# A gated graph network on one core: the z gate takes its third pass first, and the state is kept doubled

## The chip, the core and the metric

The kernel runs on one core of a Trainium2 chip. The core has a matrix engine (TensorE, PE in the profile, with its weight loads as PEld), a vector engine (VectorE, DVE), an activation engine (ScalarE, ACT), a general engine (GpSimd, POOL) and an engine that only issues transfers (SyncE, SP). TensorE writes its products into PSUM, here in eight banks of 128x512 float32; everything else lies in SBUF or in DRAM. The metric is the device time of one execution in microseconds, median of several runs.

## The reference

32 graphs of 512 nodes with 128 features each share one adjacency matrix `adj` of 512x512. Four layers follow each other, each as x = x + layer(relu(layernorm(x))). Layer 0 is a normalised graph convolution, layers 2 and 3 are graph attention. Layer 1, which the change is in, is a gated graph network of five steps:

```python
def step(h, _):
    m_in = jnp.einsum('nm,bmd->bnd', in_matrix, h)      # both matrices are adj
    m_out = jnp.einsum('nm,bmd->bnd', out_matrix, h)
    av = jnp.concatenate([m_in, m_out], axis=-1)
    u3 = h @ u3_w.T + u3_b
    z = jax.nn.sigmoid(av @ w3_w.T + w3_b + u3)
    r = jax.nn.sigmoid(av @ w4_w.T + w4_b + u3)
    hv = jnp.tanh(av @ w5_w.T + w5_b + (r * h @ u5_w.T + u5_b))
    h = (1.0 - z) * h + z * hv
    return (h, None)
```

All numbers are float32.

## The kernel before

**Products in three passes.** A float32 product would cost TensorE several passes. Most products here are made instead as three passes in a faster format (fp32r): both factors are cut into `upper` and `lower`, and a third operand `across` is made from the two (`operands`, L661 to L670: ACT makes upper at L664, DVE lower at L665 and across at L667). The first two passes add upper by upper and lower by lower into a PSUM bank. Then ACT multiplies the whole bank by SPLIT + 1 = 4097 in place (`rescale`, L672, instruction L673), and the third pass adds across by across. `in_three` (L675, passes at L691) does this for adjacency by state; `by_m` (L812, passes at L810) does it for the gates.

**A step.** `step` (L802) runs once for each graph and step, 160 times. In all but two of them the operands of the message m come in three parts ("split"). One PSUM bank serves the r gate and then the z gate: the z weights are loaded as the difference w3 - w4, so that the r gate's sum, with the part from the state in it, is the beginning of z's. After ACT has taken the tanh for r (L845), the bank is divided by 4097 (L849 and L850, an L673 instruction too), the first two passes of z follow, the bank is multiplied by 4097, the third pass follows, and ACT takes the tanh for z (L852). Sigmoids are taken as tanh of half the argument, so r and z stand here as 2 sigmoid - 1. The candidate has a bank of its own; its product with u5 (L807, a float32 product that stands as two matmul records in the profile) takes rh = (r + 1) h from L847, and u5 is halved for it. After its tanh (L856) DVE makes hv - h (L858), times z + 1 (L859), and half of that plus h (L861), the new state.

**Two layouts.** A state is needed features by nodes for the gates (hT) and nodes by features for the next adjacency product (h). Apart from the first few and the last, DVE transposes it in blocks of 32 into an `sq` tile (L642), SP writes this with four DMAs to DRAM (`far`, L645) and reads it back as whole rows (L647). The inputs of the steps (`shuttle_first`, L649) and of the attention layers go the same way. There are four sq buffers and four far buffers; the r, rh, z and hv tiles of all graphs share eight r buffers.

**Who runs when.** Nothing is written out in order. Every operation is announced to a `Plan` (L90) with its engine, a cost, a due time, the tiles that it reads and writes, and the delay until its result can be used. The plan plays this through with a limited number of buffers of each kind, always takes the most urgent operation that is ready on an engine, repeats this with other urgencies, shifts some of these by a list of numbers (`NUDGES`, L32) and then emits the instructions in that order. On the chip each engine runs its own queue in this fixed order. Six graphs (`LANES`) are in their steps at a time; the layers before and after are laid between them. [...] Two of the planned delays concern the change: the loads of x (L416) are reckoned with 3 us from their issue to the landing from the fifth graph on, and POOL's accumulating DMAs onto x (`add_onto`, L635) with 5.5.

**Normalisation.** `norm_relu` (L561) takes mean and variance on DVE (L553, L557), makes 1/sqrt(variance + eps) and -mean times this on POOL (L565 to L570), and ACT applies both with the relu (L572).

Of the kernel before, what the change touches and what calls it, by code (L numbers as in the profile page):

```python
# [32 lines left out]
    647971, 907480, 641022, 815328, 59938, 583104, 493449, 610727, 19299, 304899, 627144, 635903, 69303, 408061,  # L33
    213735, 192787, 7302, 58637, 834115, 963636, 6410, 705202, 955061, 53160, 882452, 878871, 458378, 231573,
    440371, 124696, 831158, 659333, 156550, 375431, 144007, 229366, 92171, 712320, 383813, 271697, 742240,
    798210, 397175, 163443, 123863, 724213, 516264, 896604, 122936, 743614, 457019, 570185, 62661, 920948,
    442263, 711198, 25011, 31858, 120261, 992683, 84663, 643357, 45247, 844390, 187975, 852865, 391757, 659128,
    736213, 659734, 397346, 484557, 410316, 685524, 527983, 521839, 433865, 543542, 868384, 394072, 205808,
    803310, 720274, 491124, 788541, 970038, 794737, 126558, 819621, 549318, 737826, 829243, 433351, 616176,
    868933, 314847, 688289, 939737, 907635, 853367, 672087, 953482, 982700, 636640, 260426, 745621, 974814,  # L40
    394689, 394423, 913904, 563868, 809734, 586161, 212429, 918084, 35227, 367565, 563487, 894884, 927872,
    820562, 407961, 31584, 797859, 266733, 239356, 49239, 168566, 825959, 690462, 633213, 766471, 952403,
    408935, 497281, 589831, 985192, 831666, 253050, 326020, 481827, 642272, 794393, 288155, 810682, 987219,
    726505, 745342, 441796, 26158, 800211, 187528, 795534, 149175, 951249, 42293, 197549, 962585, 253163,
    193842, 380099, 269941, 798210, 328761, 3598, 288464, 573452, 270841, 123133, 696935, 118976, 888464,
    549179, 731891, 706853, 313783, 900776, 668175, 816491, 294510, 923659, 444695, 534341, 679525, 202474,
    575303, 728118, 586387, 249556, 511121, 99992, 373622, 338542, 275589, 302881, 192606, 296189, 6121, 900716,
    93206, 158600, 419776, 382555, 10260, 855575, 704212, 698851, 696052, 457683, 55138, 404164, 139732, 866775,
    158170, 353170, 522421, 782841, 883529, 937879, 284896, 89904, 707913, 653847, 899032, 941515, 846706,
    471855, 178908, 722182, 666466, 211415, 810021, 295037, 269035, 402549, 983916, 571726, 473540, 395183,  # L50
    828707, 575084, 168839, 283291, 285134, 921509, 310987, 390552, 988218, 707221, 197452, 843224, 366926,
    884427, 545850, 986879, 832460, 861905, 777944, 317120, 973125, 261515, 931720, 503469, 106085, 519250,
    799711, 171717, 223192, 984270, 900296, 444443, 363172, 878758, 209540, 540746, 177829, 80204, 926590,
    322517, 646401, 549673, 224793, 442843, 438276, 448009, 366213, 419202, 112410, 62545, 971608, 549811,
    277513, 626388, 256930, 747343, 895280, 67763, 895530, 719737, 906641, 169362, 565633, 657856, 621526,
    269556, 28511, 630184, 65022, 38094, 940486, 350670, 532843, 24899, 947205, 540231, 223974, 479634, 329335,
    298114, 146538, 491725, 308524,
# [264 lines left out]
def gnn_stack(ctx: ExitStack, tc: tile.TileContext, a: dict, out: bass.AP):  # L322
# [13 lines left out]
    def flat(t):  # L336
# [8 lines left out]
        "sq": tiles(4, [P, Q, W * C], "sq"),  # L345
# [7 lines left out]
        "r": tiles(8, TOKENS, "r"),  # L353
# [43 lines left out]
    mhalf, eps, minus1 = (fixed(SMALL, k) for k in ("mhalf", "eps", "minus1"))  # L397
    warm = Val("r")
    op("POOL", 0.8, -1000, lambda: make_identity(nc, ident.t), w=[ident])
    for v, to in ((mhalf, -0.5), (eps, EPS), (minus1, -1.0)):  # L400
        op("POOL", 0.1, -999, lambda v=v, to=to: nc.gpsimd.memset(v.t, to), w=[v])
# [11 lines left out]
    for b in range(B):  # L413
        v = Val("x", C)
        op("SP", 0.5, -1002 if b == 0 else max(-995 + b, STEPS * b - 20) if b >= 8 else -995 + b,
           lambda v=v, b=b: nc.sync.dma_start(v.t, x[b].rearrange("(c p) d -> p c d", p=P)), w=[v], delay=(3.75, 5.2, 4.5, 5)[b] if b < 4 else 3)  # L416
        xs.append(v)
# [99 lines left out]
    gates = transposed((-9.5, -700, -700, -15.8), one(raw["u3"]), halves("w4"), halves("w3") + halves("w4", minus), halves("w5"), then=turned)  # L517
# [10 lines left out]
    u5T = transposed(-15.2, one(raw["u5"]), then=turned, by=0.5)  # L528
# [32 lines left out]
    def norm_relu(b, y, due, times=None):  # L561

        xb, off, rstd = xs[b], Val("off"), Val("rstd")
        mv = norm_stats(b, due)
        op("POOL", 0.5, due, lambda: nc.gpsimd.tensor_tensor(rstd.t, mv.t[:, :, 1], eps.t, ALU.add), r=[mv, eps], w=[rstd])  # L565
        op("POOL", 1.15, due, lambda: nc.gpsimd.tensor_tensor(rstd.t, rstd.t, mhalf.t, ALU.pow), r=[mhalf], w=[rstd])  # L566
        op("POOL", 0.42, due, lambda: nc.gpsimd.tensor_tensor(off.t, mv.t[:, :, 0], minus1.t, ALU.mult), r=[mv, minus1], w=[off])
        if times:
            op("DVE", 0.1, due, lambda: nc.vector.tensor_mul(rstd.t, rstd.t, times.t), r=[times], w=[rstd])
        op("POOL", 0.42, due, lambda: nc.gpsimd.tensor_tensor(off.t, off.t, rstd.t, ALU.mult), r=[rstd], w=[off], delay=2.6)  # L570
        for c in range(C):
            op("ACT", 0.385, due, lambda c=c: nc.scalar.activation(  # L572
                chunk(y, c), xb.t[:, c, :].rearrange("p (k j) -> p k j", k=Q) if y.kind == "h" else xb.t[:, c, :], AF.Relu, bias=off.t[:, c:c + 1], scale=rstd.t[:, c:c + 1]),
               r=[xb[c], off, rstd], w=[y[c * len(y.writers) // C]])
# [60 lines left out]
    def add_onto(x, what, reads, due):  # L635
        op("POOL", 1.0, due, lambda: nc.gpsimd.dma_start(x.t, what(), accum_op=ALU.add), r=reads, w=[x], delay=5.5)  # L636
# [147 lines left out]
    def ggnn(b, due):  # L784
        lane, h, hT = Val("lane"), Val("h" if b >= FAR0 else "y", C), Val("hT", Q)
        op("SP", 0.0, due - 3, lambda: None, r=[xs[b]], w=[lane], delay=0)
        op("SP", 0.0, due - 3, lambda: None, r=[lane], w=[h], delay=0)
        norm_relu(b, h, due - 2)
        if b >= FAR0:
            shuttle_first(h, hT, due - 2.5, due - 3)  # L790
        else:
            p = to_features(h, due - 2, hT)
            op("ACT", COPY, due - 2, lambda hT=hT: nc.scalar.copy(flat(hT.t), flat(p.t)), r=[p], w=[hT])
        for s in range(STEPS):
            now = due + LANES * s
            split = (b, s) not in WHOLE_GATES
            m = in_three(h, factors["adj"], now, split)
            if b == 4 and s == 0:
                op("SP", 0.0, now, lambda: None, r=[m[0] if split else m], w=[third], delay=0)
            h, hT = step(b, s, m, hT, now, lane)  # L800

    def step(b, s, m, hT, due, lane):  # L802
# [9 lines left out]
        def by_m(p, i, at, start, more=None, parts=None):  # L812
# [24 lines left out]
            op("PE", 2 * len(sums) * MR, at, first_two, r=[*of_gates[:2], *(v for _, three in sums for v in three[:2])], w=[p])  # L837
            rescale(p, at - 5)
            op("PE", len(sums) * MR + (MM if more else 0), at, third_one, r=[of_gates[2], *(three[2] for _, three in sums), *rest], w=[p])
# [9 lines left out]
        if split:  # L849
            rescale(gate, due - 5, 1 / (SPLIT + 1))  # L850
        by_m(gate, 2, due + 0.3, False)
        op("ACT", A, due - 5, lambda: nc.scalar.activation(flat(z.t), flat(gate.t), AF.Tanh, bias=gate_b["w3"].t, scale=0.5),  # L852
           r=[gate, gate_b["w3"]], w=[z])
        hv, new = Val("r"), Val("hT")
# [3 lines left out]
        op("DVE", V, due - 5, lambda: nc.vector.tensor_sub(flat(hv.t), flat(hv.t), flat(hT.t)), r=[hT], w=[hv])  # L858
        op("DVE", V, due - 5, lambda: nc.vector.scalar_tensor_tensor(flat(hv.t), flat(z.t), 1.0, flat(hv.t), op0=ALU.add, op1=ALU.mult),  # L859
           r=[z], w=[hv])  # L860
        op("DVE", V, due - 5, lambda: nc.vector.scalar_tensor_tensor(flat(new.t), flat(hv.t), 0.5, flat(hT.t), op0=ALU.mult, op1=ALU.add),  # L861
           r=[hv, hT], w=[new])
# [3 lines left out]
        if not EARLY <= due < STEPS * B:  # L866
            p = to_features(new, due + 2, *([] if last else [h]))
            if last:
                op("DVE", V, due + 2, lambda: nc.vector.tensor_add(flat(x.t), flat(x.t), flat(p.t)), r=[p, lane], w=[x])
            else:  # L870
                op("ACT", COPY, due + 1, lambda: nc.scalar.copy(
                    h.t.rearrange("p k (c j) -> p c k j", c=C), p.t.rearrange("p c (k j) -> p c k j", k=Q)), r=[p], w=[h])
            return h, new
        shuttle(new, "p (c q i) -> p q c i", h, due, due - 5)
        if last:
            mine = Val("y", 2)
            op("ACT", COPY, due + 2, lambda: nc.scalar.copy(
                mine.t.rearrange("p c (k j) -> p c k j", k=Q), h.t.rearrange("p k (c j) -> p c k j", c=C)), r=[h], w=[mine])
# [217 lines left out]
```

## Time and profile before

| | |
|---|---|
| median of 6 runs | 1498.71 us (1496.22 to 1501.37) |
| the profiled execution | 1496.22 us, span 1494.2 us |
| PE busy | 1486.3 us, 7464 matmul records |
| DVE busy | 1408.6 us |
| ACT busy | 1332.4 us, of which L673 466.4 us in 820 instructions of 599 ns |
| POOL busy | 447.7 us |
| DMA queues, share of 16 engines | SP's 40.6%, POOL's 16.1% |

The span runs from the first instruction to the last; the device time of the same execution is 2.0 us longer. A busy share says how long an engine had at least one instruction running. For PE it includes modelled ends, since matmuls overlap each other; the distance between the starts of matmuls in an unbroken run is the better measure of what one costs. The lists of waits name the waiting instruction, what released it, the total in us, the number of waits and the longest. PEld lines are weight loads, which run beside the matmuls. The granted clock of TensorE is at its full value from 6.3 us on to the end.

### The profile page before, as it was taken

The numbers are of one execution on the slowest core, as the hardware profiler recorded it, in microseconds if no ns is written. First come the engines' busy times: TensorE is split into PE (matmuls) and PEld (weight loads), VectorE is DVE, ScalarE is ACT, GpSimd is POOL, SyncE is SP. The second block draws the span as 40 slices with busy tenths as digits, with TensorE's granted clock in tenths as the row PEclk, the third lists the DMA queues.
The fourth block names the chain that finished last, engine by engine and source line by source line (L and its number), as shares of the span: only waits on it lengthen the run. The fifth ranks groups of instructions, "written<-read, shape, count | busy, mean of one in ns | idle before, by whom it ended". The sixth has DMA issues, their size and how long they took to land.

```text
span 1494.2 us, 25563 instructions
## 1 busy us (share of the span) xinstructions
PE 1486.3 (99%) x7464; PEld 1168.7 (78%) x7464; DVE 1408.6 (94%) x3323; ACT 1332.4 (89%) x2994; POOL 447.7 (30%) x636
## 2 busy tenths in 40 slices
PE   9999999999999999999999999999999999999999
PEld 7777777777787778777778777777777787777888
DVE  8989998999998998999999999999899999999898
ACT  6988998998989899999899989899989889989875
POOL 5411322222264223332324322333332214202321
PEclk9999999999999999999999999999999999999999
DMA  3345555745766567665665667666566565663233
GB/s 106 61 100 144 99 127 117 166 117 131 171 138 151 136 147 162 143 148 142 140 157 130 148 143 162 143 144 140 129 150 161 135 152 114 153 147 72 71 72 78
DMA packets 307499, 196.09 MB, mean 131 GB/s; under 512 B 87872, under 2 KB 259232, under 8 KB 307360
## 3 DMA queue, kind: packets, MB, share of 16 engines
q1 hardware_dynamic: 276160, 157.24, 40.6%
q0 software_dynamic: 30912, 36.71, 16.1%
q8 instruction: 59, 0.97, 0.3%
q14 instruction: 80, 0.66, 0.2%
q10 hardware_dynamic: 288, 0.52, 0.1%
HBM read 87.30 MB, written 70.37 MB: 106 GB/s over the span
## 4 chain that ended last, share of the span: by engine, by line
PE 57%; DVE 6%; DMA 1%; issue 1%; ACT 1%; SPq 0%; POOL 0%; DVEq 0%; ACTq 0%; POOLq 0%
PE bank L691 19%; PE bank L810 14%; PE bank L807 9%; PE bank L1001 9%; PE bank L932 3%; PE bank L987 1%; DVE e L975 1%; DVE lower L665 1%; PE bank L769 1%; DVE across L667 1%; DVE sq L642 0%; DMA h<-far 0%; DVE r L858 0%; DMA x<-y 0%; DVE r L859 0%
## 5 line engine op out<-in xcount | busy, mean ns | idle before, releaser
L673 ACT ACTIVATE bank<-bank 128x512 f32<-128x512 f32 x820 | 466.4, 599 | 50.5 <-PE bank L691 35.4
L667 DVE SCALAR_TENSOR_TENSOR across<-lower,upper 128x512 fp32r<-128x512 f32 x391 | 261.6, 679 | 2.4 <-PE bank L810 0.7
L810 PE MATMUL bank<-upper,gates 128*128 128x512 f32 x519 | 240.2, 463 | 0.1
L1001 PEld LDWEIGHTS bank<-h_gat,e 128*128 128x128 f32 x1792 | 220.3, 191 | 21.0 <-issue 11.7
L810 PE MATMUL bank<-across,gates 128*128 128x512 f32 x519 | 227.5, 466 | 0.6 <-ACT bank L673 0.5
L1001 PE MATMUL bank<-h_gat,e 128*128 128x129 f32 x1792 | 222.8, 275 | 0.0
L810 PE MATMUL bank<-lower,gates 128*128 128x512 f32 x519 | 205.0, 395 | 0.2 <-DVE lower L665 0.2
L691 PE MATMUL bank<-adj,across 128*128 128x512 f32 x640 | 188.3, 418 | 0.0
L691 PE MATMUL bank<-adj,upper 128*128 128x512 f32 x640 | 187.2, 414 | 0.0
L691 PE MATMUL bank<-adj,lower 128*128 128x512 f32 x640 | 175.4, 396 | 0.0
L636 POOL DMA_DIRECT2D x<-y x80 | 73.7, 929 | 313.5 <-ACT y L778 81.4
L565 POOL TENSOR_TENSOR rstd<-mv,eps 128x4 f32<-128x4 f32 x119 | 56.6, 476 | 369.8 <-DVE mv L557 361.5
L807 PE MATMUL bank<-r,wT 128*128 128x512 f32 x320 | 163.6, 593 | 0.4 <-DVE r L847 0.3
L975 DVE SCALAR_TENSOR_TENSOR e<-row,h_gat,maskT 128x512 f32<-128x512 f32 x224 | 157.3, 742 | 0.0
L566 POOL TENSOR_TENSOR rstd<-rstd,mhalf 128x4 f32<-128x4 f32 x119 | 150.6, 1266 | 1.5
L691 PEld LDWEIGHTS bank<-adj,across 128*128 128x128 f32 x640 | 117.5, 188 | 42.4 <-issue 12.5
L691 PEld LDWEIGHTS bank<-adj,upper 128*128 128x128 f32 x640 | 118.2, 188 | 37.0 <-issue 12.2
L691 PEld LDWEIGHTS bank<-adj,lower 128*128 128x128 f32 x640 | 120.5, 188 | 28.5 <-DVE lower L665 0.4
L810 PEld LDWEIGHTS bank<-across,gates 128*128 128x128 f32 x519 | 96.6, 188 | 48.4 <-ACT bank L673 19.2
L810 PEld LDWEIGHTS bank<-upper,gates 128*128 128x128 f32 x519 | 97.9, 189 | 38.0 <-issue 13.2
L845 ACT ACTIVATE r<-bank,gate_bw 128x512 f32<-128x512 f32 x160 | 111.2, 696 | 15.9 <-PE bank L807 15.5
L858 DVE TENSOR_TENSOR r<-r,hT 128x512 f32<-128x512 f32 x160 | 108.8, 681 | 15.9 <-ACT r L856 15.6
(153 smaller groups left out, 3069.7 us busy)
## 6 DMA issues: line engine op xcount, KB each, us to landing
far<-sq SPq DMA_DIRECT2D x936, 64.0 KB
h<-far SPq DMA_DIRECT2D x148, 256.0 KB
x<-y POOLq DMA_DIRECT2D x80, 256.0 KB, 4.2
sq<-far SPq DMA_DIRECT2D x56, 256.0 KB
row<-line SPq DMA_DIRECT2D x56, 256.0 KB
adjT<-y POOLq DMA_DIRECT2D x32, 256.0 KB, 4.2
hT<-far SPq DMA_DIRECT2D x120, 64.0 KB
x<-in_x_dram SPq DMA_DIRECT2D x24, 256.0 KB
```

Of the source, the lines that this page charges most:

```text
L565: op("POOL", 0.5, due, lambda: nc.gpsimd.tensor_tensor(rstd.t, mv.t[:, :, 1], eps.t, ALU.add), r=[mv, eps], w=[rstd])
L566: op("POOL", 1.15, due, lambda: nc.gpsimd.tensor_tensor(rstd.t, rstd.t, mhalf.t, ALU.pow), r=[mhalf], w=[rstd])
L636: op("POOL", 1.0, due, lambda: nc.gpsimd.dma_start(x.t, what(), accum_op=ALU.add), r=reads, w=[x], delay=5.5)
L667: op("DVE", V, due - 5, lambda: nc.vector.scalar_tensor_tensor(flat(across.t), flat(lower.t).bitcast(F32), -SPLIT, flat(upper.t).bitcast(F ...
L673: op("ACT", COPY, due, lambda: nc.scalar.mul(flat(p.t), flat(p.t), by), w=[p])
L691: nc.tensor.matmul(flat(p.t), left.t[:, c, :], right.t[:, c, :], start=first and c == 0, stop=c == C - 1, skip_group_check=True)
L807: nc.tensor.matmul(flat(p.t), (of or gates).t[:, i, :], flat(moving.t), start=start, stop=True, skip_group_check=True)
L810: nc.tensor.matmul(flat(p.t), of.t[:, i, :], flat(moving.t), start=start, stop=True, skip_group_check=True)
L845: op("ACT", A, due - 5, lambda: nc.scalar.activation(flat(r.t), flat(gate.t), AF.Tanh, bias=gate_b["w4"].t, scale=0.5), r=[gate, gate_b["w ...
L858: op("DVE", V, due - 5, lambda: nc.vector.tensor_sub(flat(hv.t), flat(hv.t), flat(hT.t)), r=[hT], w=[hv])
L975: op("DVE", 0.661, due + 3, lambda j=j: nc.vector.scalar_tensor_tensor(e.t[:, j, :], matrix(row), h.t[:, j, D + 1:D + 2], mask.t[:, j, :], ...
L1001: nc.tensor.matmul(pt()[:, c, :D + 1], e.t[:, j, i * P:(i + 1) * P], h.t[:, j, :D + 1], start=(j == 0), stop=(j == C - 1))
```

## The change

- **z gate.** `by_m` gets a form `back`: the third pass comes first, straight onto the bank as the r gate left it; the bank is then divided by 4097, the first two passes follow, and the factor that is still missing, 4097, goes into the scale of z's tanh. Each split step has three instructions of L673 in its gates where it had four.
- **State update.** kept = (z - 1) h is a DVE instruction of its own that needs z and the old state but not the candidate. After the candidate's tanh come (z + 1) hv and then -0.5 kept plus that. This sum is twice the new state in the old form, so the state h is kept doubled throughout: rstd is doubled on POOL at the entry to layer 1 (32 times), the gate weights are halved, u5 is taken with 0.25 in place of 0.5, and at the end the copy or addition onto x carries 0.5.
- **Buffers.** r from eight to nine, sq from four to three.
- **Plan.** Landings of x from the fifth graph on 8 where they were 3, accumulations 7 where they were 5.5, and another list of NUDGES, 308 numbers for 322.

Lines behind the constant list move by at most 9; the prediction names lines of the program before.

```diff
-        "sq": tiles(4, [P, Q, W * C], "sq"),
+        "sq": tiles(3, [P, Q, W * C], "sq"),
-        "r": tiles(8, TOKENS, "r"),
+        "r": tiles(9, TOKENS, "r"),
...
-           ... w=[v], delay=(3.75, 5.2, 4.5, 5)[b] if b < 4 else 3)
+           ... w=[v], delay=(3.75, 5.2, 4.5, 5)[b] if b < 4 else 8)
...
-    gates = transposed((-9.5, -700, -700, -15.8), one(raw["u3"]), ..., halves("w5"), then=turned)
+    gates = transposed((-9.5, -700, -700, -15.8), one(raw["u3"]), ..., halves("w5"), then=turned, by=0.5)
-    u5T = transposed(-15.2, one(raw["u5"]), then=turned, by=0.5)
+    u5T = transposed(-15.2, one(raw["u5"]), then=turned, by=0.25)
...
         op("POOL", 1.15, due, lambda: nc.gpsimd.tensor_tensor(rstd.t, rstd.t, mhalf.t, ALU.pow), r=[mhalf], w=[rstd])
+        if state:
+            op("POOL", 0.42, due, lambda: nc.gpsimd.tensor_tensor(rstd.t, rstd.t, two.t, ALU.mult), r=[two], w=[rstd])
...
-        op("POOL", 1.0, due, lambda: nc.gpsimd.dma_start(x.t, what(), accum_op=ALU.add), r=reads, w=[x], delay=5.5)
+        op("POOL", 1.0, due, lambda: nc.gpsimd.dma_start(x.t, what(), accum_op=ALU.add), r=reads, w=[x], delay=7)
...
+            two_of = [*of_gates[:2], *(v for _, three in sums for v in three[:2])]
+            one_of = [of_gates[2], *(three[2] for _, three in sums), *rest]
+            if back:
+                op("PE", MR, at, third_one, r=one_of, w=[p])
+                rescale(p, at - 5, 1 / (SPLIT + 1))
+                op("PE", 2 * MR, at, first_two, r=two_of, w=[p])
+                return
...
-        if split:
-            rescale(gate, due - 5, 1 / (SPLIT + 1))
-        by_m(gate, 2, due + 0.3, False)
-        op("ACT", A, due - 5, lambda: nc.scalar.activation(flat(z.t), flat(gate.t), AF.Tanh, bias=gate_b["w3"].t, scale=0.5),
+        by_m(gate, 2, due + 0.3, False, back=True)
+        op("ACT", A, due - 5, lambda: nc.scalar.activation(
+            flat(z.t), flat(gate.t), AF.Tanh, bias=gate_b["w3"].t, scale=0.5 * (SPLIT + 1) if split else 0.5),
            r=[gate, gate_b["w3"]], w=[z])
-        hv, new = Val("r"), Val("hT")
+        hv, kept, new = Val("r"), Val("r"), Val("hT")
+        op("DVE", V, due - 5, lambda: nc.vector.scalar_tensor_tensor(flat(kept.t), flat(z.t), -1.0, flat(hT.t), op0=ALU.add, op1=ALU.mult),
+           r=[z, hT], w=[kept])
         by_m(cand, 3, due + 0.4, True, (u5T, rh, [rh, u5T]))
         op("ACT", A, due - 5, lambda: nc.scalar.activation(flat(hv.t), flat(cand.t), AF.Tanh, bias=gate_b["w5"].t),
            r=[cand, z, gate_b["w5"]], w=[hv])
-        op("DVE", V, due - 5, lambda: nc.vector.tensor_sub(flat(hv.t), flat(hv.t), flat(hT.t)), r=[hT], w=[hv])
         op("DVE", V, due - 5, lambda: nc.vector.scalar_tensor_tensor(flat(hv.t), flat(z.t), 1.0, flat(hv.t), op0=ALU.add, op1=ALU.mult),
            r=[z], w=[hv])
-        op("DVE", V, due - 5, lambda: nc.vector.scalar_tensor_tensor(flat(new.t), flat(hv.t), 0.5, flat(hT.t), op0=ALU.mult, op1=ALU.add),
-           r=[hv, hT], w=[new])
+        op("DVE", V, due - 5, lambda: nc.vector.scalar_tensor_tensor(flat(new.t), flat(kept.t), -0.5, flat(hv.t), op0=ALU.mult, op1=ALU.add),
+           r=[hv, kept], w=[new])
```

The constant list NUDGES, the new tile `two` that holds 2.0, and the 0.5 at the last step (in L869 and L877) are left out here.

## The prediction

> **What bounds the kernel now.** First the page's head and its first part, busy time by engine:
>
> ```profile
> span 1494.2 us, 25563 instructions
> PE 1486.3 (99%) x7464; PEld 1168.7 (78%) x7464; DVE 1408.6 (94%) x3323; ACT 1332.4 (89%) x2994; POOL 447.7 (30%) x636
> ```
>
> TensorE (PE) reads as full, but the ends of matmuls are modelled, so a full row alone proves nothing. The chain that ended last gives the spacing of matmuls in unbroken runs (start, us, what):
>
> ```profile
> 515.78 1.86 PE bank L691 x8
> ...
> 528.81 2.68 PE bank L1001 x24
> ...
> 1017.96 2.09 PE bank L810 x9
> ```
>
> A 128x512 fp32r pass takes 1.86/8 = 0.2325 us, the same on L691 and L810 (2.09/9 = 0.232); a 128x129 fp32 one 2.68/24 = 0.112 us. The fp32 pair of L807 follows from the timeline near 601 us:
>
> ```profile
> 601.36 1.02 PE L807 MATMUL bank<-hT,wT 128*128 128x512 f32 x2
> 601.81 0.80 PE L810 MATMUL bank<-across,gates 128*128 128x512 f32 x1
> 602.45 1.02 PE L807 MATMUL bank<-hT,wT 128*128 128x512 f32 x2
> ```
>
> From pair to pair 1.09 us pass, and one fp32r pass is in it, so each of the two costs (1.09 - 0.2325)/2 = 0.43 us. Now the work in the span: L691 640*3 + 112*3 = 2256 and L810 519*3 = 1557 fp32r passes, 3813 x 0.2325 = 886.5; L1001 and L987 2048 x 0.112 = 229; L807 562 x 0.43 = 242; L932 512 and L769 256 at 0.112 = 86; transposes, the first layer's products and the set-up together about 36. Sum 1479 us. PE's first matmul starts at 1.06 and its last ends near 1490.5, so only 10 us of idle are left for anything to win; adding up the recorded starts that come later than the end of the matmul before gives 12.7. Of these 5.6 lie in the first 30 us and 7.1 are strewn over the rest, none longer than 0.75. PE's waits name causes:
>
> ```profile
> PE bank L769 <- ACT m L717: 0.7, 2, 0.5
> PE bank L631 <- ACT y L616: 0.6, 1, 0.6
> PE bank L810 <- ACT bank L673: 0.5, 2, 0.3
> ```
>
> The reader is to see tenths of a microsecond here, against 466 us that ScalarE (ACT) spends on the rescalings of L673. From 1490.5 to 1494.2 VectorE (DVE) and the last store run alone: 3.7 us.
>
> **The change, part by part.**
>
> *One rescaling fewer.* 158 of the 820 L673 instructions go (the order of the new program has 662). At 0.599 us that is 94.6 us of ACT, 1332 to 1238. All of it lies beside PE. On the path it is worth what PE waited for ACT bank L673, 0.5 us by the modelled ends; bounds 0 and the 7.1 us of strewn idle.
>
> *Third pass first.* PE's passes are the same 1557. The third pass now waits for the r tanh (L845) where the two passes waited for tanh and rescaling; then one rescaling and two passes. Handovers between PE and ACT stay four; one ACT instruction drops out, 0.6 us of latency. In the new order the PE work between a pass and the next one across a rescaling has a median of 3.4 us for the r and candidate gates (before 2.8) and 2.3 for z, at least 0.9 (before 0.5): the 0.6 us rescaling stays covered by other graphs' matmuls. Cost 0.
>
> *kept = (z - 1) h.* DVE's count is unchanged: 160 subtractions at 0.681 go (L858), 160 scalar-tensor-tensors at the 0.679 of L859 come. Zero by itself. After the candidate's tanh two DVE instructions follow instead of three, 0.68 us less in a loop whose shortest closing (from the candidate's last matmul to the same graph's next adjacency pass) holds 19.1 us of PE work in the old order and 17.7 in the new: the plan has spent the gain on a tighter loop. The new wait is kept's on z's tanh; behind it on DVE stand other graphs' operands (L665, L667). The old order paid this for r, and pays it for the subtraction whose place the multiply takes:
>
> ```profile
> DVE r L858 <- ACT r L856: 15.6, 22, 2.6
> DVE r L847 <- ACT r L845: 10.6, 16, 1.9
> DVE st L553 <- DMA x<-in_x_dram: 12.7, 8, 3.9
> ```
>
> So kept may add 10 to 16 us of DVE waiting at most, of 86 us that DVE is idle anyway; at least nothing. It is hidden where DVE is ahead of PE: the operand of L665 is ready 3.05 us (median, from the recorded times) before its adjacency pass starts, 1.5 at the tenth percentile. I take 0.
>
> *Longer landings in the plan.* Nothing is issued more; normalisations are placed later behind their x. Of the 12.7 us in the last line 3.9 fall at the start, where the four loads keep their times. The other 8.8 us should go; next late would be the accumulations (L636), planned at 7 and landing in 4.2 to 5.2. PE gaps follow two such stalls (0.26 us at 413.6, 0.12 at 474.7), so 0.5 us on the path, with 0 and 8.8 as ends.
>
> *Doubled state.* 32 POOL multiplies of 128x4 in the chain rstd, off: at the 0.41 to 0.56 us of the rows of L567 and L570, 15 us of POOL, 30% busy. In SP's queue nothing is added. Behind the multiply stand off's product and four relus; only graphs 0 and 1, whose first step has little beside it, can show it: 0 to +0.5 each, I take +0.5 in all. The 28 copies of L877 become multiplications by 0.5, both ACT at 0.63, and the four adds of L869 keep their 0.68: 0.
>
> *sq from four buffers to three, r from eight to nine.* A trip holds its sq buffer from the transposition until the four DMAs have read it; up to the issue that closes it this took 6.0 us in the median over the 234 trips, 8.1 at the ninetieth percentile, 10.9 at most. Between two transpositions into one buffer the old order has 16.9 us of DVE work (median) and 4 of 185 below 8 us; the new one 12.2 and 23. SP waits for the landings 81.1 us over 91 issues, at most 2.8 each, so a landing comes 2 to 3 us after the last issue where the plan reckons 4, and the short distances mostly hold. Price between 0 and the rival below; I take 0.
>
> *Idle transposes.* The seven of L372 go (order: 7 to 0), with the 0.58 us hole they surround:
>
> ```profile
> 1445.88 0.60 PE L372 MATMUL bank<-ident 128*128 128x128 f32 x4
> ...
> 1447.18 0.55 PE L631 MATMUL bank<-ident,y 128*128 128x128 f32 x3 [0.58 <-ACT y L616]
> ```
>
> 7 x 0.109 + 0.58 = 1.3 us, if the new tail has work there; bounds 0 and 1.3. The last 20 rows of PE's order are alike in kind and spacing, so the 3.7 us at the end stay.
>
> [...]
>
> *Sum.* Profiled execution 1496.2 us (span 1494.2 and 2.0 around it). Rescaling 0.5, landings 0.5, tail 1.3, and half of the other 5 us or so of strewn idle, 2.5, since ACT has 95 us more room; against +0.5 on POOL: -4.3. The profiled one was the fastest of six, 2.5 below the median of 1498.7; taking the same distance again: 1498.7 - 4.3 = 1494.4.
>
> **The rivals.**
>
> *Full anyway.* The new order has its own small holes, PE's idle stays at 10 to 13 us, and 95 us of ACT vanish unseen. For it: PE's work is the same to 0.8 us. Against it: more distance at the rescalings. 1497 to 1500, say 1498.
>
> *Three sq buffers stop DVE (slower).* The transposition waits for a slow far write, and all of DVE behind it. Place: the 23 short distances. Price: a hold of 8.1 to 10.9 us against a distance of 6 to 8 is a wait of some 3 us; less the lead of 1.5 to 3 us that PE's operands have, up to 1.5 us reach PE. If one in three of the 23 meets a long hold, 8 x 1.5 = 12 us, less the gain of 4.3: 1506. It decides from 4.3 + 3.0 = 7.3 us on PE, five such waits. Against it: no wait of the old trace stands between a transposition and a far write.
>
> *Every strewn hole closes.* All 7.1 go and runs scatter less: 1490.
>
> **How the numbers follow.** 0.2% is 3.0 us, about what a measurement can tell from no change. Forecast (1492 to 1496.5) 0.42, full anyway 0.32, sq 0.16, every hole 0.10. Faster: nine tenths of the forecast and the last, less a little, 0.48; same: the rest of the forecast and nearly all of full anyway, 0.34; slower 0.18, with the tail of full anyway. The range leaves out half of the last and two thirds of sq's: 1489 to 1503; the forecast's own is 1492 to 1496.5.
>
> **What would show it.** Right: L673 x662 near 397 us, ACT about 83%, DVE still near 1409, PE's work unchanged, strewn idle of 2 to 5 us, st L553 waiting under 3 us for in_x_dram after the start. Wrong: DVE sq L643 waiting for far<-sq by more than 10 us in all, kept's line on DVE waiting above 16, or PE holes above 1 us in mid-span.

## The result, and the profile after

The changed kernel took 1501.91 us (median of 20 runs, 1498.57 to 1505.62) beside 1497.44 us (41 runs, 1495.05 to 1501.37) for the kernel before on the same chip: ratio 1.0029, 95% interval 1.0023 to 1.0035. It is 4.5 us slower where 4.3 us faster was forecast. Lines below are those of the changed program (L674 is the rescaling, L692 the adjacency passes, L811 the passes of the gates).

The page of the changed kernel, its head, the busy times and the row of the rescaling:

```profile
span 1496.0 us, 25469 instructions
PE 1487.1 (99%) x7457; PEld 1169.4 (78%) x7457; DVE 1407.7 (94%) x3323; ACT 1263.8 (84%) x2836; POOL 445.9 (30%) x669
L674 ACT ACTIVATE bank<-bank 128x512 f32<-128x512 f32 x662 | 378.9, 596 | 88.2 <-PE bank L692 65.4
```

ACT has lost 69 us of busy time for the 94.6 forecast, and PE has gained 0.8 with seven matmuls fewer. This execution took 1497.79 us, less than any of the 20 timed ones: it alone does not show the loss. Its waits of DVE and of PE:

```profile
DVE r L862 <- ACT r L858: 12.6, 15, 2.7
DVE sq L643 <- ACT y L573: 8.6, 10, 2.0
...
DVE st L552 <- DMA x<-in_x_dram: 4.1, 2, 4.0
```

```profile
PE bank L941 <- DMA sq<-far: 1.5, 1, 1.5
```

The reader is to see what is missing: no wait of the transposition L643 for a far write, and no wait of PE for a rescaling. Read in this way the change had done what it says, but for the first line of PE's waits. That line is a hole of 1.5 us at 283 us, where an attention layer's matmul waits for a read-back from DRAM; the prediction had named holes of over 1 us in mid-span as a sign of being wrong. Two more things, which no list of waits of this profile names, had moved: the distance between matmuls, and a stretch of GpSimd between 35 and 44 us that came out in two ways.

Sums of PE's idle from here on count from the recorded end of a matmul, which is modelled, to the next recorded start. The kernel before has 3.3 us by that count, 2.1 of them behind the first 30 us (and behind 100, since none lies between); the prediction's count, with earlier ends, had 12.7 and 7.1.

### The profile page after: what moved, and what is told of

Read it like the earlier page. It is cut to its first block, busy times and chain, and to the rows that moved or that the text cites. A ratio compares the mean times of both kernels' runs of the same rounds, so it can differ in the third digit from the quotient of the medians.

```text
span 1496.0 us, 25469 instructions
## 1 busy us (share of the span) xinstructions
PE 1487.1 (99%) x7457; PEld 1169.4 (78%) x7457; DVE 1407.7 (94%) x3323; ACT 1263.8 (84%) x2836; POOL 445.9 (30%) x669
## 4 chain that ended last, share of the span: by engine, by line
PE 95%; DVE 3%; DMA 1%; ACT 0%; issue 0%; SPq 0%; ACTq 0%; DVEq 0%
PE bank L692 34%; PE bank L811 24%; PE bank L808 16%; PE bank L1010 13%; PE bank L941 3%; PE bank L770 2%; DVE e L984 1%; PE bank L715 1%; PE bank L996 1%; DMA sq<-far 0%; PE bank L632 0%; DMA e<-in_adj_dram 0%; DMA h<-far 0%; DVE x L1025 0%; DVE lower L666 0%
## 5 line engine op out<-in xcount | busy, mean ns | idle before, releaser
L674 ACT ACTIVATE bank<-bank 128x512 f32<-128x512 f32 x662 | 378.9, 596 | 88.2 <-PE bank L692 65.4
L811 PE MATMUL bank<-upper,gates 128*128 128x512 f32 x519 | 245.8, 474 | 0.0
L811 PE MATMUL bank<-across,gates 128*128 128x512 f32 x519 | 220.3, 462 | 0.0
L811 PE MATMUL bank<-lower,gates 128*128 128x512 f32 x519 | 205.1, 395 | 0.6 <-DVE lower L666 0.6
L692 PE MATMUL bank<-adj,upper 128*128 128x512 f32 x640 | 189.4, 417 | 0.0
L692 PE MATMUL bank<-adj,across 128*128 128x512 f32 x640 | 186.1, 416 | 0.0
L692 PE MATMUL bank<-adj,lower 128*128 128x512 f32 x640 | 175.8, 396 | 0.0
L692 PEld LDWEIGHTS bank<-adj,across 128*128 128x128 f32 x640 | 117.4, 188 | 40.1 <-issue 8.8
L692 PEld LDWEIGHTS bank<-adj,upper 128*128 128x128 f32 x640 | 118.4, 188 | 38.7 <-issue 12.8
L692 PEld LDWEIGHTS bank<-adj,lower 128*128 128x128 f32 x640 | 120.4, 188 | 29.4
L565 POOL TENSOR_TENSOR rstd<-rstd,mhalf 128x4 f32<-128x4 f32 x119 | 138.5, 1164 | 1.4
L811 PEld LDWEIGHTS bank<-upper,gates 128*128 128x128 f32 x519 | 97.9, 189 | 40.7 <-issue 13.9
L811 PEld LDWEIGHTS bank<-across,gates 128*128 128x128 f32 x519 | 96.3, 189 | 41.9 <-issue 11.5
L811 PEld LDWEIGHTS bank<-lower,gates 128*128 128x128 f32 x519 | 97.8, 189 | 37.3 <-issue 17.9
```

The source lines that it names most:

```text
L674: op("ACT", COPY, due, lambda: nc.scalar.mul(flat(p.t), flat(p.t), by), w=[p])
L692: nc.tensor.matmul(flat(p.t), left.t[:, c, :], right.t[:, c, :], start=first and c == 0, stop=c == C - 1, skip_group_check=True)
L811: nc.tensor.matmul(flat(p.t), of.t[:, i, :], flat(moving.t), start=start, stop=True, skip_group_check=True)
```

## The experiments

Each set of runs had a chip of its own, so times are compared with those of the kernel before in the same set.

### The two kernels once more, and a fourth sq buffer

> The program before, unchanged, once more, for a second profile. Both theories: 1495 to 1501 us, and TensorE's idle between its first and last matmul within 4 us of the 12.7 us of the first profile.

> The changed program, unchanged, once more, because its first profile (1497.8 us) is faster than every one of its 20 timed runs. Theory of the holes: an ordinary run of 1500 to 1504 us shows 3 to 8 us more TensorE idle than the first profile's 12.5 us, in a few holes of over 1 us that end at a transfer or at an instruction behind one. Theory of the clock: the idle is the same and the clock record shows 6 us or more at half clock before TensorE's last matmul.

e1 gives the plan's three sq buffers a fourth one without letting the plan use more than three at a time, so that the order of work stays. To make room, some set-up tiles are laid inside the new one:

```diff
-        "sq": tiles(3, [P, Q, W * C], "sq"),
+        "sq": tiles(3, [P, Q, W * C], "sq") + [spare],
...
-                short = [v for v in opens if len(free[v.kind]) < sum(...)]
+                short = [v for v in opens if len(free[v.kind]) - (v.kind == "sq") < sum(...)]
```

> The changed program with a fourth sq buffer and otherwise the same order of instructions on every engine: the plan still counts with three, but the tile that it hands out is the one that has been free longest of four. The fourth tile's room comes from set-up tiles that are laid into it. Theory of the three sq buffers (the slower rival of the prediction): 1497 to 1499 us, since each transposition then finds a buffer that has been free for some 5 us more. Theory that something else in the new order loses the time: 1501 to 1503 us, as the changed program.

e2 is the changed kernel with `NUDGES = ()`, the plan's order before the list of shifts.

> The changed program with an empty list NUDGES, so the order that the plan finds by itself. If the change as such is worth nothing and the lists alone decide: 1512 to 1520 us, as the program before would be without its list. If the change as such saves time and its list fits the chip worse than the old list did: 1505 to 1511 us.

The profiled executions took 1500.00 us (before) and 1500.04 (after). e1: 1497.45 us, ratio to before 0.9988 (0.9978 to 0.9999). e2: 1500.98, ratio 1.0017 (1.0008 to 1.0026), under both of its expectations. So without its list of shifts the changed kernel is slower than the kernel before too (which had its own), and the fourth buffer seemed to bring the loss back. But e1's strewn idle after 100 us is that of e0_after_again (2.1 and 1.8 us). Both have the same matmuls in the same order, so the start of each can be set beside that of its twin: the difference grows evenly by 4.7 us from 100 to 1400 us. That is no wait but a rate.

The second profile of the kernel before is 3.7 us longer than its first, by holes alone. The largest follows a load of x that lands late (DVE, then PE):

```profile
414.45 0.49 DVE L553 BATCH_NORM_STATS2 st<-x 128x6 f32<-128x128 f32 x2 [3.71 <-DMA x<-in_x_dram]
...
415.58 1.12 PE L807 MATMUL bank<-r,wT 128*128 128x512 f32 x2 [1.75 <-DVE r L847]
```

So executions of the kernel before scatter too, and a single profile of either kernel is no measure of the difference.

The second execution of the changed kernel has 6.2 us of PE idle for the first one's 4.0, less than the 3 to 8 more that the theory of the holes asked for, and no stretch at half clock, as the theory of the clock asked for (its mean granted clock is 1.0). It differs from the first in one main place. Matmul by matmul it falls 3.3 us behind between 30 and 50 us; 0.9 of that comes back at 283 us, where its hole is 0.6 us for 1.5. Its timeline of VectorE and GpSimd (start, us, engine and line):

```profile
35.08 0.67 DVE L666 TENSOR_TENSOR lower<-y,upper 128x512 fp32r<-128x512 f32 x1
...
38.66 1.29 DVE L477 TENSOR_TENSOR an<-an,an 128x512 fp32r<-128x512 f32 x2
39.86 0.38 DVE L556 BATCH_NORM_AGGREGATE mv<-st 128x2 f32<-128x6 f32 x4
...
35.31 4.70 POOL L568 TENSOR_TENSOR off<-mv,minus 128x4 f32<-128x4 f32 x1 [1.02 <-DVE mv L556]
39.97 0.20 POOL L564 TENSOR_TENSOR rstd<-mv,eps 128x4 f32<-128x4 f32 x1
40.24 3.25 POOL L565 TENSOR_TENSOR rstd<-rstd,mhalf 128x4 f32<-128x4 f32 x1
...
44.17 0.49 ACT L573 ACTIVATE y<-x,off,rstd 128x128 f32<-128x128 f32 x1 [3.47 <-POOL off L571]
...
45.20 1.20 PE L692 MATMUL bank<-adj,across 128*128 128x512 f32 x4 [1.20 <-ACT bank L674]
48.05 1.20 PE L692 MATMUL bank<-adj,across 128*128 128x512 f32 x4 [1.65 <-ACT bank L674]
```

The same GpSimd operations in the first execution:

```profile
35.41 0.49 POOL L568 TENSOR_TENSOR off<-mv,minus 128x4 f32<-128x4 f32 x1 [1.02 <-DVE mv L556]
35.85 0.65 POOL L564 TENSOR_TENSOR rstd<-mv,eps 128x4 f32<-128x4 f32 x1
36.58 1.33 POOL L565 TENSOR_TENSOR rstd<-rstd,mhalf 128x4 f32<-128x4 f32 x1
```

A multiply of 4 columns took 4.70 us here and 0.49 there, with the same instructions on VectorE beside it. The long one ends at 40.01 us, 0.15 us after VectorE, behind eight operations with two inputs and no gap from 35.08 on, has started one with a single input (39.86). This is the normalisation of graph 4 in layer 0; ACT waits 3.47 us for its result, with two rescalings behind it in its queue, and PE has two holes. PE's waits have it too:

```profile
PE bank L692 <- ACT bank L674: 2.9, 2, 1.6
```

Such operations are not new with the change. The profile before has thirteen GpSimd operations of over 2 us among those of 128x4, which the means of the prediction's rows hide; the longest lasts through eight VectorE operations with two inputs in the same way (to 1240.65, the transposition behind them starts at 1240.50) and comes back in all four profiles with that order, with no hole of PE near it:

```profile
1235.76 4.89 POOL L570 TENSOR_TENSOR off<-off,rstd 128x4 f32<-128x4 f32 x1
```

```profile
1235.69 0.69 DVE L667 SCALAR_TENSOR_TENSOR across<-lower,upper 128x512 fp32r<-128x512 f32 x1
...
1240.50 0.71 DVE L642 STREAM_TRANSPOSE sq<-hT 128x512 f32<-128x512 f32 x1
```

The first two profiles of the changed kernel have four each. What is new is the place, early in the run, where PE has holes behind them.

Of the nine profiles with this order of work and nothing set against the effect, six have the 4.70 (e0_after_again, e1, e3, e4, e6, e8) and 4.3 to 5.0 us of PE idle in the first 100 us; three have 0.49 (the first, e7, e13) and 1.4 to 2.0. All five of them whose tiles were moved are among the six, and of the four with the changed kernel's own addresses one; whether the addresses or the chips have a part in that was not tested. In e1 the holes were followed by a granted clock of 0.54 from 48 to 51 us and 0.69 from 51 to 52 (windows; PEclk stands behind POOL):

```profile
45.00:48.00 3.00, 1.19 (x4) 0.67 (x4) 1.61 (x5) 2.97 (x7) 1.43 (x3) 1.00 0.57 110
48.00:51.00 3.00, 2.69 (x5) 1.83 (x6) 1.88 (x4) 2.36 (x6) 0.91 (x1) 0.54 0.87 109
51.00:52.00 1.00, 1.00 (x3) 0.53 (x2) 1.00 (x4) 1.00 (x4) 0.00 (x0) 0.69 0.45 50
```

### Addresses, and small operations between

e3 lays the tiles as e1 does, with three sq buffers: the spare tile is there and holds the set-up tiles, but is no sq buffer.

> The changed kernel's order of work with three sq buffers, but with its tiles at the SBUF addresses that they had with the fourth buffer (the moving tiles adj and an 832 bytes further up, those of the gates 1888). Theory that the gain of the run with four buffers came from the addresses: adj passes at 230.7 ns and gate passes at 233.6 ns as there, the strewn idle time of TensorE as in the changed kernel, and 1497.5 us (1496 to 1499), some 4.5 us under the changed kernel. Theory that the fourth buffer brought it: 233.4 and 232.6 ns as in the changed kernel, and 1501 to 1502.5 us.

e4 only moves the 16 bytes of the new tile `two` behind all others:

```diff
-    mhalf, eps, minus1, two = (fixed(SMALL, k) for k in ("mhalf", "eps", "minus1", "two"))
+    mhalf, eps, minus1 = (fixed(SMALL, k) for k in ("mhalf", "eps", "minus1"))
+    two = Val(None)
...
+    two.t = tiles(1, SMALL, "two")[0]
     with tc.manual_schedule():
```

> The changed kernel with the new tile of 16 bytes laid out last instead of ahead of the factors, so that adj, an and the gates start at the kernel before's addresses plus nothing (32 bytes lower than in the changed kernel). Theory that the spacing of the matmuls follows the address: adj passes fall from 233.45 ns to some 232.6, 2256 passes x 0.85 = 1.9 us, 1500.0 us (1499 to 1501). Theory that the spacing follows the state tiles or chance: 233.4 ns and 1501.5 to 1502.5 us.

e5 puts `nc.vector.bn_stats(tick.t, ident.t[:, :8])` behind each of the eight operations that make the an factors (L474, L477).

> The changed kernel, its addresses untouched, with a VectorE statistic of 8 columns (one input, some 0.1 us) behind each of the eight operations that make the an factors, in the stretch from 35 to 45 us in which VectorE issued seven operations with two inputs in a row and GpSimd's multiply of 0.5 us took 4.7. Theory that GpSimd waits there until VectorE comes to an operation with one input: off<-mv falls from 4.70 to under 2.5 us, the power from 3.25 to under 2.5, the relu of graph 4 starts 2 to 3 us earlier, TensorE's holes of 1.4 and 1.8 us at 45 and 48 us go, and the time is 1498 to 1500 us (2 to 4 under the changed kernel, whose median has these holes), with less scatter. Theory that the length of the GpSimd operations has another cause, or that the holes do not set the time: GpSimd's operations stay over 4 us or the time stays at 1501 to 1502.5 us.

e6 lays empty tiles of 32 to 192 bytes ahead of the factors (none of adj1):

```diff
+    PADS = {"gates1": 128, "gates2": 64, "gates3": 32, "adj2": 32, "adj3": 160, "an1": 160, "an2": 64, "an3": 192}
```

> The changed kernel with empty tiles of 32 to 192 bytes between the factors, so that the distance from the weights' address to the moving tile's, modulo 512 bytes, is 128, 160 and 320 for the three adj tiles, 352 (128 and 256 by the next) for an, and 64, 0 and 480 for the gates. Theory that the spacing of the fp32r passes follows this distance: a different mean spacing for each of the nine tiles, between 229 and 235 ns, the same within 0.3 ns wherever the distance is the same; the total within 10 us of the changed kernel either way. Theory that the distance has nothing to do with it: all within 0.3 ns of 233.4 (adj) and 232.6 (gates). an1 is at 352, an2 at 416 and an3 at 96 if the padding adds up as laid out; the profile's records are read by the addresses.

Kernel before in this set: 1497.27 us. e3: 1492.95, ratio 0.9973 (0.9961 to 0.9985), better still than the e1 that it copies, so the fourth buffer brought nothing. e4: 1497.67, ratio 1.0001 (0.9991 to 1.0012): with 16 bytes moved nothing is left of the loss. That is more than the 1.9 us expected, but the changed kernel was timed on another chip, and its loss turned out to differ between chips (below). e5: 1499.36, ratio 1.0017 (1.0008 to 1.0027); the changed kernel was not timed beside it, so its time does not settle what the small operations saved. e6, one execution: 1495.55.

The mean distance from the start of one fp32r pass to that of the next, worked out from the recorded starts after 60 us (distances of 150 to 300 ns; adj and an together, then the gates), is:

```
kernel                      adj starts at  adj+an ns   gates start at  ns
                            (mod 2048)                 (mod 512)
before                      1024           232.6       416             232.5
after, e0_after_again       1056           233.5       448             232.6
e1, e3                      1920           230.7       288             233.7
e4 (16 bytes last)          1024           232.6       416             232.4
e12 (before + 16 bytes)     1056           233.3       448             232.8
e8, e9 (after, placed)      1920           229.5        64             230.6
e10 (before, placed)        1920           229.6        64             230.5
e6: adj1 1280 231.3, adj2 1312 232.3, adj3 1472 232.2; an1 1664 230.5, an2 1728 232.7, an3 1920 232.2
```

The profile shows no addresses; these follow from the sizes of the tiles in the order in which they are laid. an starts 32 bytes further than adj (mod 2048), except in e8, e9 and e10, where both start at 1920, and in e6. Taken apart, the address goes with the distance from tile to tile: the lower-by-lower passes take 234.2 ns with adj at 1056 in the changed kernel, and 234.2 with an at 1056 in the kernel before.

The order of work shows no part in it: the same address gives nearly the same distance in the programs before and after (adj+an with adj at 1024: 232.6 in both; at 1056: 233.3 and 233.5; at 1920, placed: 229.6 and 229.5). Nor is any wait in it, since these are distances in unbroken runs. e6's tiles range over 230.5 to 232.7 ns rather than 229 to 235. That alone proves little, since the three adj tiles of the kernel before, all at 1024, differ by nearly as much (231.7, 233.5, 232.1); but in the changed kernel the same six have 233.2, 234.2, 233.4 and 232.5, 232.7, 232.4, so four of the six shrink by over 1 ns. Which property of the address decides (the remainder by 512 or 2048, the distance to the weights) is not settled, and adj's remainder alone does not: at 1920 adj has 230.3 ns in e1 and 229.4 in e8. The gates at 64 and the adj tiles at 1920 do best, that is all.

In e5 GpSimd's long multiply ends at an operation with one input, put there for it. Its timeline:

```profile
37.30 0.18 DVE L478 BATCH_NORM_STATS2 tick<-ident 128x6 f32<-128x8 f32 x1
...
39.91 0.18 DVE L485 BATCH_NORM_STATS2 tick<-ident 128x6 f32<-128x8 f32 x1
...
42.66 0.73 DVE L660 STREAM_TRANSPOSE sq<-h 128x512 f32<-128x512 f32 x1
...
35.16 2.29 POOL L575 TENSOR_TENSOR off<-mv,minus 128x4 f32<-128x4 f32 x1 [1.03 <-DVE mv L563]
37.41 0.71 POOL L571 TENSOR_TENSOR rstd<-mv,eps 128x4 f32<-128x4 f32 x1
38.21 2.00 POOL L572 TENSOR_TENSOR rstd<-rstd,mhalf 128x4 f32<-128x4 f32 x1
40.29 2.53 POOL L578 TENSOR_TENSOR off<-off,rstd 128x4 f32<-128x4 f32 x1
```

The 4.70 became 2.29 and ends within the first small operation. A new long one (2.53) stands between 40.29 and the transposition at 42.66, where no small operation was laid; the hole at 45 us is gone, the one at 47 stays.

In these timelines the four long multiplies (4.70, 4.89, 2.29 and 2.53 us) end 0.15 or 0.16 us after VectorE has started an operation with one input; the long powers (3.25 and 2.00) end 0.96 and 0.22 us after the start of one. What holds them up is not shown by any run, and the two inputs alone do not settle it: the 4.70 lasted through eight such VectorE instructions, and beside the same ones the first execution has 0.49.

### Both at once

e8 lays the changed kernel's factors so that gates start at 64 (mod 512) and adj and an at 1920 (mod 2048); e10 does it to the kernel before (40 floats in the first tile); e9 is e8 with the small operation behind each of the eleven two-input operations of 35 to 42 us; e7 is the changed kernel as it is.

```diff
+        tiles(1, [P, 32], "pad_gates")
         upper, lower, across = [fixed([P, 4, P], "gates" + k, dtype=F32R) for k in ("1", "2", "3")]
...
+            dinv2 = fixed(SMALL, "dinv2")
+            tiles(1, [P, 176], "pad_adj")
             factors["adj"] = factors_of(adjT, "adj", -3.6, ys[0])
...
             o.emit()
+            if o.engine == "DVE" and o.cost >= 0.575 and 33 < o.at < 41.5:
+                self.between()
```

> The changed kernel as it is, timed beside the three others of this set on one chip: 4.4 us over the kernel before (3.5 to 5), as when its result was taken; adj passes at 233.5 ns and gate passes at 232.6.

> The changed kernel, its order of work untouched, with two empty tiles and dinv2 laid out ahead of the factors, so that the moving tiles adj and an start 256 bytes (modulo 512) from the weights and the gates at 64. Theory that the spacing of the fp32r passes follows the addresses: adj 229.8 ns (233.5 before, 1920 passes, 7.0 us), an 231.4 (0.5 us), gates 230 to 232 (1 to 4 us): 8 to 11 us under the changed kernel, 4 to 7 under the kernel before, with the holes at 45 and 48 us still there. Theory that the earlier gains had another cause: the time of the changed kernel within 1.5 us.

> The kernel laid out anew, with a VectorE statistic of 8 columns behind each of the eleven operations with two inputs of the stretch from 35 to 42 us. Theory of the wait of GpSimd for an operation with one input: no GpSimd operation over 2 us between 35 and 44 us, no hole of TensorE over 0.5 us between 43 and 50 us, 3 us under the same kernel without them (2 to 4), and less scatter. Theory that the holes cost nothing in the end or have another cause: the same within 1 us.

> The kernel before, its order of work untouched, with the same placing of the gates, adj and an. Theory of the addresses: adj from 232.6 to 229.8 ns (5.4 us), an from 233.9 to 231.4 (0.8 us), gates from 232.5 to 230 to 232 (1 to 4 us): 7 to 10 us under the kernel before. Against the changed kernel with this placing, what is left of the change itself: if the new order with its late GpSimd operations costs 2 to 3 us and brings the 1.5 us of the forecast, the kernel before is 0.5 to 2 us the faster of the two; if addresses were all that slowed the changed kernel, it is 1 to 2 us the slower.

Kernel before: 1498.25 us (17 runs). e7: 1497.62, ratio 1.0006 (0.9993 to 1.0018), in two groups: eight runs at 1496.4 to 1498.4, four at 1500.6 to 1504.2. e8: 1490.62, 0.9946 (0.9931 to 0.9960), 7.0 us under e7 where 8 to 11 were expected. e9: 1488.06 (1487.62 to 1488.26), 0.9931 (0.9919 to 0.9943). e10: 1493.45 (1490.88 to 1494.44), 0.9963 (0.9950 to 0.9977). The same run of 36 passes in the chains of the changed kernel and of e8 (start, us, what):

```profile
451.47 8.43 PE bank L692 x36
```

```profile
452.00 8.19 PE bank L693 x36
```

8.43/36 = 234.2 ns and 8.19/36 = 227.5 ns: 0.24 us here, and the kernel has 3813 such passes. e9's page and its GpSimd:

```profile
span 1486.2 us, 25480 instructions
PE 1476.8 (99%) x7457; PEld 1168.0 (79%) x7457; DVE 1405.8 (95%) x3334; ACT 1262.2 (85%) x2836; POOL 442.7 (30%) x669
```

```profile
35.54 0.49 POOL L571 TENSOR_TENSOR off<-mv,minus 128x4 f32<-128x4 f32 x1 [1.02 <-DVE mv L559]
35.99 0.71 POOL L567 TENSOR_TENSOR rstd<-mv,eps 128x4 f32<-128x4 f32 x1
36.78 1.40 POOL L568 TENSOR_TENSOR rstd<-rstd,mhalf 128x4 f32<-128x4 f32 x1
```

No GpSimd operation is late (none over 1.52 us from 34 to 47 us), no hole is left at 45 us, and the five timed runs lie within 0.7 us, where e8's six lie within 5. That is the fastest version: 10 us under the kernel before. From the changed kernel to e8 the distances shrink by 4.0 ns x 2256 + 2.0 ns x 1557 = 12.1 us; the span shrinks by 9.0 (1498.3 to 1489.3, both with late GpSimd operations), the median by 7.0 (e7 to e8). e7 itself missed its 4.4 us over the kernel before. e10's 3.0 x 2256 + 2.0 x 1557 = 9.9 us brought 4.8, under the 7 to 10 expected. Beside the first profile before, matmul by matmul, the stretches that begin with a pass of adj or an are 6.4 us shorter in all, as they should be; those that begin with a pass of the gates, waits included, are 0.8 us longer. Why the gates' part did not come is open.

### The two causes one by one

e11 is the changed kernel at its own addresses with the eleven small operations; e12 is the kernel before with an unused tile, `tiles(1, SMALL, "two")`, laid where the change lays its own; e13 is the changed kernel.

> The changed kernel at its own addresses with the eleven small VectorE operations between 35 and 42 us, and nothing else. If the late GpSimd operations are the whole of the step between its two groups of times (1496.4 to 1498.4 and 1500.6 to 1504.2 beside a kernel before of 1498.2), only the lower group is left: 0.5 to 1.5 us under the kernel before, within 1 us from run to run, no GpSimd operation over 2 us from 35 to 44 us. If the step has another cause, both groups stay. By the forecast's sum less the spacing (4.3 - 1.9) it is 2.4 us under.

> The kernel before, its order of work untouched, with an unused tile of 16 bytes laid out where the change lays out its own, so that the gates, adj and an start 32 bytes further up, as in the changed kernel. Theory that the spacing follows the addresses: adj passes from 232.6 to 233.45 ns, 1.6 us over the kernel before (1 to 2.5). Theory that the spacing is a matter of the order of work: 232.6 ns and the same time.

> The changed kernel beside the two on their chip, since the share of its executions that have the late GpSimd operations was 16 of 20, and then 4 of 12 on another chip: two groups of times, 2 to 4 us apart; the lower group within 1 us of the run with the small operations, the upper 2 to 6 us over it.

Kernel before: 1496.14 us (27 runs). e12: 1498.89, ratio 1.0011 (1.0003 to 1.0020). e11: 1497.70, 1.0012 (1.0003 to 1.0021). e13: 1498.56, 1.0013 (1.0002 to 1.0024), of which nine runs at 1496.4 to 1499.9 and two at 1501.9 and 1503.5. The tile alone, with not an instruction changed, slows the kernel before by as much as the whole change does on this chip. Matmul by matmul, e12 falls behind the first profile before evenly, from nothing at 100 us to 2.0 at 1400.

e11 (1496.5 to 1500.0) lies 0.7 us under the lower group of e13: where late executions are rare, the small operations take off little but the upper end. Two of e13's eleven runs lie in the upper group and none of e11's eleven, too few to show it by the times. The small operations do not bring the changed kernel under the kernel before, as they should have by 0.5 to 2.4 us; e12 says that 0.11% of what is left is addresses.

## Why the prediction was wrong

The sign was wrong. The sum lacked two costs, each of which can be found in a sentence of the prediction, and part of the gain that it counted on did not show.

- **"3813 x 0.2325 = 886.5."** This is the step that failed, and e12 and e4 show it. The prediction read the distance of fp32r passes off the program before and carried it over to a program whose tiles lie elsewhere. The 16 bytes of `two` take 32 of the partition (in the built programs the tiles of that size lie 32 bytes apart), adj, an and the gates move up by 32, and 2256 passes x 0.85 ns = 1.9 us are lost. e12 loses 1.7 us (0.11%; 2.75 by the medians) without the change, and e4 has the old distance back.
- **The sum, "half of the strewn idle".** It holds no new hole, and *Doubled state* looked only at graphs 0 and 1 and at the added multiply, with GpSimd's durations taken from the means (0.41 to 0.56 us), though single ones took up to 4.89. The new order puts the normalisation of graph 4 beside eight two-input operations; where its 0.49 us becomes 4.70, PE starts the matmuls behind it 3.3 us later. 17 of the 20 runs of the result lie above 1500.8 and three at 1498.6, as e7's two groups do. That these 17 are the late ones is argued from the profiles, which show both kinds; the timed runs have no trace. Which kind comes, and why the share of the upper group differed from set to set (17 of 20, 4 of 12, 2 of 11), stays open.
- **One rescaling fewer.** Right on the count and the wait: 662 of 596 ns, ACT at 84% for the forecast's 83, and PE's wait of 0.5 us for it is gone from the first profile. ACT's own gain was mis-sized: 820 x 599 ns is 491 us, but the row is busy 466.4, since instructions overlap at their ends, and 68.6 us went for 94.6.
- **Third pass first, kept.** No wait of PE for a rescaling stands in the first profile, as forecast. kept's line waits 12.6 us, inside the 10 to 16 named.
- **Longer landings.** The wait went from 12.7 to 4.1 us as forecast. The 0.5 us was priced by two small gaps of one profile; the second profile before has 15.7 us of this wait and the hole of 1.75 us, so it can be worth more in some executions.
- **Idle transposes.** Right: the seven of L372, which the plan of the kernel before laid where it found TensorE idle near its end, are gone, 0.76 us of work, and PE's idle behind 1400 us went from 0.74 to 0.43. The granted clock of the changed kernel is 1.00 without them from 1440 us to the last matmul.
- **Strewn holes.** Not found as forecast. Behind 100 us PE's idle is 2.1 and 5.2 us in the two profiles before and 1.6 to 3.0 in the four of the changed kernel, so the 2.5 us forecast are more than the faster profile before had to give. The hole at 283 us is in all twelve profiles of the new order, with 0.3 to 1.5 us; the four of the old order have at most 0.3 of this wait.
- **The rivals.** *Three sq buffers stop DVE* had the right sign and the wrong cause: no transposition waited more than 0.2 us for a far write, SP's waits for landings rose only from 81.1 to 90.4 us, and with three buffers e3 was no slower than e1 with four. The hole at 283 us is there with four buffers too (0.8 us in e1). What planning with three costs through the order was not tested. *Full anyway* was closest to the chips where late executions are rare (1497.6 and 1498.6). None of the four cases held a change in TensorE's own rate.

Between 4.3 us faster and 4.5 slower lie 8.8 us. The addresses account for 1.9. Late GpSimd operations in 17 of 20 runs would add 17/20 x 3.3 = 2.8, an estimate. The other 4 are gain that was forecast and did not show. What the change brings at equal addresses and without late GpSimd operations is, from e12 to e11, 1.2 us by the medians (1498.89 to 1497.70), 1.7 by the profiled executions, nothing by the ratios; from e10 to e9 it is 5.4 us (1493.45 to 1488.06; five runs each) and 3.3 by the profiled executions. The forecast's 4.3 lies between; the runs do not settle it closer, so whether the terms of the gain were mis-sized, and which, stays open.

## What to carry to other kernels

Here an unused tile of 16 bytes ahead of TensorE's operands took the distance between passes of adj and an from 232.6 to 233.3 ns and the time up by 0.11% (e12), with TensorE 99% busy. Where TensorE is full, look at the addresses of the matmul operands before and after, and try a pad before tuning an order. Beside eight VectorE operations with two inputs a GpSimd multiply on a critical chain took 4.70 us in six profiles of nine, 0.49 in the other three: look for such places in a new order. A small VectorE operation with a single input in between cost 0.08 us of VectorE (e5, 37.30 to 37.38 us), and eleven of them saved 2.6 us here (e8 to e9). Look at the longest durations of a row and not only at its mean. When executions fall into two groups, one profile shows one of them: take a second before explaining the median.

## What the runs showed of the hardware

- The distance between 128x512 fp32r passes moved with the place of their operands in SBUF: between runs of one order of work in which nothing but tiles was moved it is 229.5 (e8) to 233.5 ns (e0_after_again) on average for adj and an, and 230.6 (e8) to 233.7 (e1, e3) for the gates, with 7457 matmuls and as many weight loads in each.
- A GpSimd multiply of 128x4 took 4.70 us beside eight VectorE instructions with two inputs (e0_after_again) and 0.49 beside the same ones (the first profile).
- Two holes of TensorE, 3.0 us together between 40 and 51 us, were followed in e1 by a granted clock of 0.54 (48 to 51 us) and 0.69 (51 to 52 us), with 1.00 ahead and behind. In e0_after_again and e3, where the same wait is 2.9 us, the mean granted clock of the whole execution is 1.0.
